# A convolution kernel with paired rows: the order of its two half sums, who normalises a few images, and where a denser pattern begins

## The chip, the cores and the metric

The kernel runs on one core of a Trainium2 chip. The metric is the device time of one execution in microseconds (us), median of several executions. All runs told here were in the fast state of the machine, and fast runs are compared with fast runs. A ratio is the mean time of one kernel's fast runs over the mean time of the other's fast runs of the same rounds, so it is not quite the ratio of the medians that are quoted. Where parts of the span are compared, the times are from one profiled execution of each kernel.

## The reference, cut to what matters

160 images of 128 channels and 32 x 32 pixels are normalised in groups of four channels, convolved 3 x 3 with weights of five sets (quantised on the fly), and added to the input.

```python
w = (v1 + v2).reshape(OUT_CH * N, IN_CH, K, K)          # two-step quantised U
...
act = jax.lax.conv_general_dilated(xb, w, window_strides=(1, 1),
          padding=[(1, 1), (1, 1)], feature_group_count=N, ...)
...
x = x + _L0_conv_ref(_gn(x), L0_conv_U)                 # _gn: 32 groups, eps 1e-5
```

## The kernel before

The precision of fp16 products is restored by two parts, a high and a low one, of each normalised image. Rows are taken in pairs, so that some products serve two rows: the sum half (`m[:, 0]`) and the difference half (`m[:, 1]`) of an image are multiplied first, into two banks of PSUM (the memory that TensorE writes its products to). A tile, below, is one buffer as the program allots it; here one tile, m, holds both banks. ScalarE copies the difference half out (`leave`), VectorE writes their sum and difference as the beginning of even and odd rows (`pairs`), and TensorE adds the remaining products on top (`rest_of_column`). "Combined" images form their row combinations in fp32 before they are split into parts; this saves TensorE products and costs VectorE work.

```python
def sums_of_pairs(self, i):
    m = self.m[i] = self.banks(self.ps_m, "m", i)      # ps_m has one buffer: two banks
    both = self.both(i)
    for a, kind in enumerate((self.SUM, self.DIFF)):
        for col in self.COLS:
            for j, (_, st) in enumerate(both):
                self.product(m[:, a], i, kind, st[:, a], col, ...)

def conv(self, i, on_the_way):
    if self.FIRST < i < self.imgs - 1:
        self.sums_of_pairs(i + 1)                      # the next image's halves
    ...                                                # then the rest of image i

def leave(self, i):
    m2 = self.evac.tile([self.P, self.H // 2, self.W], F32, tag="m2", name=f"m2_{i}")
    self.nc.scalar.copy(m2, self.m[i][:, 1])
    self.m[i] = self.m[i], m2

def pairs(self, i, between=lambda: None):
    m, m2 = self.m.pop(i)
    eo = self.eo[i] = self.banks(self.ps_eo, "eo", i)
    rows = eo.rearrange("p h (i a) w -> p (h i) a w", a=2)
    nc.vector.tensor_add(rows[:, :, 0], m[:, 0], m2)
    between()
    nc.vector.tensor_sub(rows[:, :, 1], m[:, 0], m2)

def combined(self, i):
    ...
    return (i - self.STEADY) % 7 % 2 == 0 if i < self.THIRDS else i % 3 != 1   # THIRDS = 126

def by_vector_too(self, i):                            # VectorE normalises in ScalarE's place
    if i < self.STEADY + 4 or i >= self.imgs or self.combined(i):
        return False
    return i >= self.THIRDS or (i - self.STEADY) % 7 == 3
```

Of the kernel before, what the change touches and what calls it, by code (L numbers as in the profile page):

```python
# [8 lines left out]
F32 = mybir.dt.float32  # L9
# [24 lines left out]
class Steps:  # L34


    def __init__(self, nc, pool):
        self.nc = nc
        self.pool = pool
        self.s1, self.s2, self.lift = (self.col(tag) for tag in ("s1", "s2", "lift"))  # L40
        self.parts1, self.parts2 = (
            tuple(self.col(tag + part) for part in ("r", "n", "nhi", "nlo"))
            for tag in ("s1", "s2")
        )
        self.far = self.col("fari", I32)
# [264 lines left out]
class Main:  # L310
# [25 lines left out]
    LOAD_LEAD = 18  # L336
    STEADY = 7
    BY_VECTOR = (8, 10, 11, 14, 19, 24, 29, 34)
    THIRDS = 126
    EARLY = 8  # L340
    FIRST = 3

# [4 lines left out]
    def __init__(self, tc, ctx, keep, x, u, out):  # L347
        nc = self.nc = tc.nc
        self.imgs, C, self.H, self.W = x.shape
        P = self.P = nc.NUM_PARTITIONS  # L350
        assert C == P and self.H * self.W == 1024
        self.per_set = self.imgs // N_SETS
        self.xv = x.rearrange("(b n) c h w -> n c b (h w)", n=N_SETS)
        self.ov = out.rearrange("(b n) c h w -> n c b (h w)", n=N_SETS)
        self.uv = u.rearrange("n (o i k) -> n o i k", o=C, k=TAPS)

        def pool(name, bufs, **kw):
            return ctx.enter_context(tc.tile_pool(name=name, bufs=bufs, **kw))

        self.const = pool("const", 1)  # L360
        self.qpool = pool("quant", 1)
        self.wpool = pool("weights", 2)
        self.upool = pool("u", 1)
        self.xpool = pool("x", 11)
        self.zpool = pool("z", 3)
        self.parts = pool("parts", 5)
        self.rows = pool("rows", 4)
        self.wide = pool("wide", 2)
        self.wide_parts = pool("wide_parts", 3)
        self.evac = pool("evac", 2)  # L370
        self.sums = pool("sums", 3)
        self.unread = pool("unread", 1)
        self.small = pool("small", 3)
        self.ps_eo = pool("ps_eo", 2, space=PSUM)
        self.ps_m = pool("ps_m", 1, space=PSUM)
        self.ps_stat = pool("ps_stat", 1, space=PSUM)
        self.ps_tr = pool("ps_tr", 1, space=PSUM)
        self.steps = Steps(nc, keep)
        self.chunks, self.z, self.hi, self.v, self.eo, self.m = {}, {}, {}, {}, {}, {}
        self.sum = {}  # L380
        self.wts = {}
        self.step = 0
        self.columns = []

        cuts = [0, 2, 4, 8, 12, 16, 20, *range(24, self.imgs + 1, 8)]
        self.groups = [range(a, b) for a, b in zip(cuts, cuts[1:])]
        self.group_of = {i: k for k, g in enumerate(self.groups) for i in g}
        self.stats = {}
# [135 lines left out]

    def by_vector_too(self, i):

        if i < self.STEADY + 4 or i >= self.imgs or self.combined(i):
            return False
        return i >= self.THIRDS or (i - self.STEADY) % 7 == 3

    def high_part(self, i):
        hi = self.parts.tile([self.P, self.H, self.W], MM, tag="hi", name=f"hi{i}")
# [3 lines left out]
    def combined(self, i):  # L536
# [3 lines left out]

        return (i - self.STEADY) % 7 % 2 == 0 if i < self.THIRDS else i % 3 != 1

# [94 lines left out]
                    skip_group_check=True,  # L637
                )

    def banks(self, pool, tag, i):  # L640
        return pool.tile([self.P, 2, self.H // 2, self.W], F32, tag=tag, name=f"{tag}{i}")

    def warm_up(self, count):


        zeros = self.los[3].rearrange("p h w -> p (h w)")
        if "warm" not in self.m:
            self.m["warm"] = self.banks(self.ps_m, "m", "warm")
        for _ in range(count):
            self.nc.tensor.matmul(  # L650
                self.m["warm"][:, 0].rearrange("p i w -> p (i w)"), zeros[:, :128],
                zeros[:, :512], start=True, stop=True,
            )

    def direct_hi(self, i, col):

        if i not in self.eo:
            self.eo[i] = self.banks(*((self.ps_eo, "eo") if i < 2 else (self.ps_m, "m")), i)
        self.taps(i, (self.hi[i], 0), col, self.eo[i], False)

    def direct_lo(self, i, col):
# [19 lines left out]

    def sums_of_pairs(self, i):

        m = self.m[i] = self.banks(self.ps_m, "m", i)
        both = self.both(i)
        for a, kind in enumerate((self.SUM, self.DIFF)):
            for col in self.COLS:
                for j, (_, st) in enumerate(both):
                    self.product(
                        m[:, a], i, kind, st[:, a], col,  # L690
                        col == self.COLS[0] and j == 0,
                        col == self.COLS[-1] and j == len(both) - 1,
                    )
# [30 lines left out]
    def leave(self, i):  # L724

        m2 = self.evac.tile([self.P, self.H // 2, self.W], F32, tag="m2", name=f"m2_{i}")
        self.nc.scalar.copy(m2, self.m[i][:, 1])  # L727
        self.m[i] = self.m[i], m2

    def pairs(self, i, between=lambda: None):  # L730


        nc = self.nc
        m, m2 = self.m.pop(i)
        eo = self.eo[i] = self.banks(self.ps_eo, "eo", i)
        rows = eo.rearrange("p h (i a) w -> p (h i) a w", a=2)
        nc.vector.tensor_add(rows[:, :, 0], m[:, 0], m2)  # L737
        between()
        nc.vector.tensor_sub(rows[:, :, 1], m[:, 0], m2)  # L739

    def by_hand(self, i):

# [336 lines left out]
```

## Time and profile before

| | before |
|---|---|
| median of 3 runs | 1057.07 us |
| span of the profiled run | 1053.8 us |
| TensorE / VectorE / ScalarE busy | 91 / 90 / 84% |
| images 17 to 24, profiled | 53.1 us |
| images 24 to 126 | 633.0 us, 6.21 an image |
| images 126 to 146 | 124.0 us |
| images 146 to 159 | 82.8 us |

Images are counted by ScalarE's copies of the difference half, one per image from image 3 on: "images 17 to 24" runs from the copy of image 17 to that of image 24. No engine is full, and the waits between them form a ring; the prediction shows the lines and reads them.

### The profile page before, as it was taken

How to read it: one execution, taken by the hardware profiler on the slowest of the kernel's cores; microseconds unless marked ns; L12 is line 12 of the kernel's file. 1: busy time of each engine (PE TensorE's matmuls, PEld its weight loads, DVE VectorE, ACT ScalarE, POOL GpSimd, SP SyncE). 2: the span in 40 equal slices, each digit the busy share in tenths (PEclk: the TensorE clock that was granted, in tenths of full speed). 3: DMA queues.
4: the chain of work that ended last, by engine and by line, in shares of the span. 5: the costliest groups of instructions: out<-in, count | busy, mean ns of one | idle time of the engine just before them, and what ended most of it. 6: DMA issues, size and time to landing. Idle time of an engine off the chain costs nothing.

```text
span 1053.8 us, 16029 instructions
## 1 busy us (share of the span) xinstructions
PE 955.8 (91%) x5935; PEld 574.3 (54%) x5935; DVE 943.6 (90%) x1264; ACT 883.2 (84%) x1202; POOL 439.8 (42%) x603
## 2 busy tenths in 40 slices
PE   1989998799999899999999999999999999898996
PEld 1445555455655556555555555555555555555554
DVE  7999997998899999889999998899999988889885
ACT  4879897789889998998998989988999888877451
POOL 3446653343515271635343544416162623243430
PEclk9999999899999999999999999999999999999999
DMA  9438899789999989999899999999999899997764
GB/s 361 172 101 240 239 241 264 205 230 239 280 257 244 258 242 264 258 278 268 257 241 261 251 258 256 278 255 242 264 264 254 238 262 260 252 242 200 178 160 143
DMA packets 67287, 254.42 MB, mean 241 GB/s; under 512 B 5248, under 2 KB 5248, under 8 KB 67200
## 3 DMA queue, kind: packets, MB, share of 16 engines
q1 hardware_dynamic: 45168, 173.09, 48.6%
q0 software_dynamic: 22032, 80.23, 39.4%
q8 instruction: 48, 0.79, 0.3%
q14 instruction: 39, 0.32, 0.1%
HBM read 89.19 MB, written 83.89 MB: 164 GB/s over the span
## 4 chain that ended last, share of the span: by engine, by line
PE 45%; DVE 33%; ACT 11%; issue 4%; POOL 4%; DMA 2%; SPq 0%; POOLq 0%; ACTq 0%; DVEq 0%
PE m L669 20%; PE eo L631 16%; PE eo L669 6%; DVE vl L584 6%; DVE eo L737 5%; DVE eo L739 5%; DVE v L567 4%; ACT vh L578 3%; ACT junk L199 3%; DVE v L570 3%; DVE v L573 2%; ACT m L727 2%; DVE lo L591 2%; DMA xt<-sum 1%; ACT sum L753 1%
## 5 line engine op out<-in xcount | busy, mean ns | idle before, releaser
L669 PEld LDWEIGHTS <-wt 128*128 128x128 f16 x4464 | 432.8, 98 | 311.8 <-DVE eo L739 74.9
L766 POOL DMA_DIRECT2D xt<-sum x153 | 138.3, 904 | 443.3 <-ACT sum L753 433.7
L631 PE MATMUL eo<-hi,wt 128*128 128x496 f16 (+3 forms) x1224 | 292.4, 376 | 1.1 <-ACT wt L477 0.6
L669 PE MATMUL m<-vh,wt 128*128 128x512 f16 x546 | 209.9, 384 | 60.3 <-DVE eo L739 60.2
L584 DVE SCALAR_TENSOR_TENSOR vl<-v,rstd,vh 128x2048 f16<-128x2048 f32 x91 | 213.6, 2347 | 0.4 <-ACT vh L578 0.3
L669 PE MATMUL eo<-vh,wt 128*128 128x256 f16 (+1 forms) x1092 | 209.3, 273 | 0.0
L669 PE MATMUL eo<-vl,wt 128*128 128x256 f16 (+1 forms) x1092 | 209.3, 273 | 0.0
L669 PE MATMUL m<-vl,wt 128*128 128x512 f16 x546 | 209.3, 383 | 0.0
L631 PEld LDWEIGHTS <-wt 128*128 128x128 f16 x1296 | 126.4, 99 | 124.2 <-ACT wt L477 1.8
L578 ACT ACTIVATE vh<-v,rstd 128x2048 f16<-128x2048 f32 x91 | 182.7, 2007 | 4.9 <-POOL v L557 4.0
L737 DVE TENSOR_TENSOR eo<-m,m 128x512 f32<-128x512 f32 x157 | 109.2, 696 | 82.3 <-ACT m L727 82.0
L753 ACT ACTIVATE sum<-eo 128x1024 f32<-128x1024 f32 x153 | 154.6, 1011 | 26.4 <-PE eo L669 25.6
L192 ACT ACTIVATE junk<-xt 128x1024 f16<-128x1024 f32 x152 | 160.7, 1057 | 17.3 <-DMA xt<-in_x_dram 14.3
L199 ACT ACTIVATE junk<-xt,mv 128x1024 f16<-128x1024 f32 x152 | 173.8, 1143 | 0.2
L727 ACT COPY m<-m 128x512 f32<-128x512 f32 x157 | 91.4, 582 | 96.0 <-PE m L669 95.2
L669 PE MATMUL eo<-rows,wt 128*128 128x248 f16 (+1 forms) x792 | 119.1, 273 | 0.0
L739 DVE TENSOR_TENSOR eo<-m,m 128x512 f32<-128x512 f32 x157 | 108.8, 693 | 1.2
L567 DVE TENSOR_TENSOR v<-xt 128x960 f32<-128x960 f32 x91 | 104.7, 1150 | 0.0
L669 PE MATMUL m<-rows,wt 128*128 128x496 f16 (+1 forms) x396 | 96.5, 380 | 0.8 <-DVE eo L739 0.8
L591 DVE TENSOR_TENSOR lo<-z,hi 128x1024 f16<-128x1024 f32 x69 | 84.5, 1224 | 0.7 <-POOL twice L244 0.7
L557 POOL TENSOR_SCALAR v<-xt,ngm 128x32 f32<-128x32 f32 x91 | 82.5, 907 | 0.0
L556 POOL TENSOR_SCALAR v<-xt,ngm 128x32 f32<-128x32 f32 x91 | 80.3, 883 | 0.0
(112 smaller groups left out, 895.4 us busy)
## 6 DMA issues: line engine op xcount, KB each, us to landing
xt<-in_x_dram SPq DMA_DIRECT2D x78, 1024.0 KB, 8.9
out_dram<-xt SPq DMA_DIRECT2D x78, 1024.0 KB, 5.1
xt<-sum POOLq DMA_DIRECT2D x153, 512.0 KB, 6.7
range<-in_L_conv_U_dram SPq DMA_DIRECT2D x4, 576.0 KB, 7.8
u<-in_L_conv_U_dram SPq DMA_DIRECT2D x4, 576.0 KB, 11.8
xt<-in_x_dram SPq DMA_DIRECT2D x4, 512.0 KB, 10.2
out_dram<-xt SPq DMA_DIRECT2D x3, 512.0 KB, 2.7
u<-in_L_conv_U_dram SPq DMA_DIRECT2D x2, 288.0 KB, 3.0
```

The source lines that it names most:

```text
L192: self.nc.scalar.activation(junk, image, ACTF.Copy, scale=-1.0 / image.shape[1], accum_out=self.mv[:, j, 0:1],)
L199: self.nc.scalar.activation(junk, image, ACTF.Square, bias=self.mv[:, j, 0:1], accum_out=self.mv[:, j, 1:2],)
L567: nc.vector.tensor_sub(v[:, W:last], x[:, : last - W], x[:, 2 * W :])
L578: self.nc.scalar.mul(vh, self.v[i], st.rstd[:, j])
L584: self.nc.vector.scalar_tensor_tensor(vl, self.v[i], st.rstd[:, j], self.hi[i], ALU.mult, ALU.subtract)
L631: nc.tensor.matmul(target[:, h, r0 - h0 : r1 - h0, c0:c1], self.wts[n, col][:, k, :], tile[:, s0 : s0 + r1 - r0, c0 + dw : c1 + dw], start ...
L669: self.nc.tensor.matmul(target[:, :, c0:c1], self.wts[n, col][:, kind, :], source[:, :, c0 + dw : c1 + dw], start=start, stop=stop, skip_g ...
L727: self.nc.scalar.copy(m2, self.m[i][:, 1])
L737: nc.vector.tensor_add(rows[:, :, 0], m[:, 0], m2)
L739: nc.vector.tensor_sub(rows[:, :, 1], m[:, 0], m2)
L753: nc.scalar.mul(self.sum[i], eo, 0.5)
L766: self.nc.gpsimd.dma_start(self.image(i), self.sum.pop(i), accum_op=ALU.add)
```

## The change

Its intent, as one reads it from the diff: the two banks of m become one lasting tile, so that no new buffer is allotted for each image, and the difference half is multiplied first. The copy can then run while the sum half is multiplied, and the next difference half can begin once the copy is through. Beside it, two parts of the schedule: images that begin a statistics group are normalised by ScalarE, and so are all the remaining ones from image 146; and the pattern of two combined images in three begins at image 146, not 126.

```diff
-    THIRDS = 126
+    THIRDS = 146
...
+        self.pair = self.ps_m.tile([P, 2, self.H // 2, self.W], F32, tag="m", name="m")
...
-        if i < self.STEADY + 4 or i >= self.imgs or self.combined(i):
+        if not self.STEADY + 4 <= i < self.THIRDS or (i - self.STEADY) % 7 != 3:
             return False
-        return i >= self.THIRDS or (i - self.STEADY) % 7 == 3
+        return i != self.groups[self.group_of[i]].start
...
-        m = self.m[i] = self.banks(self.ps_m, "m", i)
+        m = self.pair
         both = self.both(i)
-        for a, kind in enumerate((self.SUM, self.DIFF)):
+        for a, kind in ((1, self.DIFF), (0, self.SUM)):
...
-        self.nc.scalar.copy(m2, self.m[i][:, 1])
+        self.nc.scalar.copy(m2, self.pair[:, 1])
...
-        nc.vector.tensor_add(rows[:, :, 0], m[:, 0], m2)
+        nc.vector.tensor_add(rows[:, :, 0], m1, m2)          # m1 = self.pair[:, 0]
```

More of the change, by code (lines that the diff above doesn't have):

```diff
@@ L378, in __init__ @@
         self.steps = Steps(nc, keep)
-        self.chunks, self.z, self.hi, self.v, self.eo, self.m = {}, {}, {}, {}, {}, {}
+        self.pair = self.ps_m.tile([P, 2, self.H // 2, self.W], F32, tag="m", name="m")
+        self.chunks, self.z, self.hi, self.v, self.eo, self.m2 = {}, {}, {}, {}, {}, {}
         self.sum = {}
@@ L638, in taps, with bank_pair @@
                 )
-    def banks(self, pool, tag, i):
-        return pool.tile([self.P, 2, self.H // 2, self.W], F32, tag=tag, name=f"{tag}{i}")
+    def bank_pair(self, i):
+        return self.ps_eo.tile([self.P, 2, self.H // 2, self.W], F32, tag="eo", name=f"eo{i}")
     def warm_up(self, count):
         zeros = self.los[3].rearrange("p h w -> p (h w)")
-        if "warm" not in self.m:
-            self.m["warm"] = self.banks(self.ps_m, "m", "warm")
         for _ in range(count):
             self.nc.tensor.matmul(
-                self.m["warm"][:, 0].rearrange("p i w -> p (i w)"), zeros[:, :128],
+                self.pair[:, 0].rearrange("p i w -> p (i w)"), zeros[:, :128],
                 zeros[:, :512], start=True, stop=True,
@@ L657, in direct_hi @@
         if i not in self.eo:
-            self.eo[i] = self.banks(*((self.ps_eo, "eo") if i < 2 else (self.ps_m, "m")), i)
+            self.eo[i] = self.bank_pair(i) if i < 2 else self.pair
         self.taps(i, (self.hi[i], 0), col, self.eo[i], False)
@@ L726, in leave @@
         m2 = self.evac.tile([self.P, self.H // 2, self.W], F32, tag="m2", name=f"m2_{i}")
-        self.nc.scalar.copy(m2, self.m[i][:, 1])
-        self.m[i] = self.m[i], m2
+        self.nc.scalar.copy(m2, self.pair[:, 1])
+        self.m2[i] = m2
     def pairs(self, i, between=lambda: None):
         nc = self.nc
-        m, m2 = self.m.pop(i)
-        eo = self.eo[i] = self.banks(self.ps_eo, "eo", i)
+        m1, m2 = self.pair[:, 0], self.m2.pop(i)
+        eo = self.eo[i] = self.bank_pair(i)
         rows = eo.rearrange("p h (i a) w -> p (h i) a w", a=2)
-        nc.vector.tensor_add(rows[:, :, 0], m[:, 0], m2)
+        nc.vector.tensor_add(rows[:, :, 0], m1, m2)
         between()
-        nc.vector.tensor_sub(rows[:, :, 1], m[:, 0], m2)
+        nc.vector.tensor_sub(rows[:, :, 1], m1, m2)
     def by_hand(self, i):
```

## The prediction

> **What bounds the kernel now.** I read the busy shares first, then the waits of the steady stretch, then one turn of the loop in the timeline, then the three late stretches, and last the half-clock stretch near the start. In the fences the page comes first, then the waits of 201.8 to 834.8 us (images 24 to 126), then the timeline, then busy time by stretch.
>
> ```profile
> PE 955.8 (91%) x5935; PEld 574.3 (54%) x5935; DVE 943.6 (90%) x1264; ACT 883.2 (84%) x1202; POOL 439.8 (42%) x603
> L739 DVE TENSOR_TENSOR eo<-m,m 128x512 f32<-128x512 f32 x157 | 108.8, 693 | 1.2
> L521 DVE TENSOR_SCALAR z<-xt,rstd,shift 128x1024 f32<-128x1024 f32 x27 | 21.9, 812 | 3.9 <-POOL shift L242 3.9
> ```
>
> ```profile
> DVE eo L737 <- ACT m L727: 49.6, 56, 1.7
> ...
> ACT m L727 <- PE m L669: 37.3, 52, 1.6
> ...
> PE m L669 <- DVE eo L739: 32.4, 25, 1.7
> ```
>
> ```profile
> 407.45 0.57 ACT L727 COPY m<-m 128x512 f32<-128x512 f32 x1
> ...
> 408.06 0.70 DVE L737 TENSOR_TENSOR eo<-m,m 128x512 f32<-128x512 f32 x1 [0.34 <-ACT m L727]
> ...
> 409.00 0.69 DVE L739 TENSOR_TENSOR eo<-m,m 128x512 f32<-128x512 f32 x1
> ...
> 409.74 0.39 PE L669 MATMUL m<-vh,wt 128*128 128x512 f16 x1 [1.39 <-DVE eo L739]
> ```
>
> ```profile
> 150.00:200.00 50.00, 41.07 (x239) 23.47 (x237) 42.47 (x65) 37.85 (x52) 17.37 (x25) 0.90 0.94 262
> ...
> 201.80:834.80 633.00, 598.13 (x3762) 362.45 (x3761) 582.06 (x764) 579.26 (x789) 276.53 (x365) 1.00 0.95 253
> 834.80:958.80 124.00, 112.23 (x724) 69.93 (x723) 108.83 (x125) 107.07 (x144) 39.33 (x62) 1.00 0.94 249
> 958.80:1053.80 95.00, 81.50 (x526) 50.66 (x523) 72.72 (x84) 40.00 (x42) 28.85 (x36) 0.98 0.61 167
> ```
>
> No engine is full: TensorE, VectorE and ScalarE are at 94, 92 and 92% of the long stretch, and the DMA engines at 0.95. The waits close a ring. TensorE waits to write m until VectorE's second pair operation has read it; VectorE waits for ScalarE's copy of half of m; ScalarE waits for TensorE to finish that half. The timeline shows one turn: copy, add, subtract, and only then the first matmul of the next m, 1.39 us late. So a latency ring through one pair of PSUM banks binds, with all engines close behind it. In the steady stretch there are two such stops of 1.0 to 1.7 us in every seven images, which take 43.7 us (successive large pieces of the chain begin at 299.59, 343.34 and 387.10 us); in the later pattern of three images, 18.8 us, one of 1.6 to 1.8 us.
>
> **What the Trainium skill says.** "PSUM — Partial Sum Buffer", section "PSUM bank collisions raise a hardware error", asks that accesses be guarded by bank and quadrant. The two halves of m are 512 fp32 columns each, one bank each, so the sum half and the difference half may be released separately. The trace of before shows them released together: the first matmul of m waits for the last reader of either. "Perfetto Trace Analysis", section "Identifying the Most-Contended Engine", calls a repeating gap a sign of too little PSUM for the next tile; the repeating stop agrees. "DMA: Bandwidth & Descriptors", section "Issuing engines are not separate DMA queues": all transfers share 16 engines; the share of 0.95 is the warning here. "TensorE: Matmul & The Clock Gate", section "What's actually happening": an idle window of about 3.4 us halves the clock. In the 150 to 200 us window the granted clock is 0.90 and two runs of twelve product matmuls take 4.45 and 4.13 us in the chain instead of 2.61 or 2.77; the gaps near them are 2.8 and 6.0 us, so the trace agrees roughly.
>
> **The change part by part.** *Order and buffer.* Durations are start to start in the timeline and the chain. TensorE: m takes 2.6 us for a combined image (12 matmuls), 1.3 for another (6); the rest takes 2.6 (24 half matmuls) or 5.15 (three times 1.27 + 0.44). Per seven images (4 combined, 3 not): 4 x 5.2 + 3 x 6.45 = 40.15 us, and 40.8 busy with the statistics' and weights' matmuls. VectorE: low part of a combined image 2.26, its combining 1.06 + 0.66 + 0.60 = 2.3; low part and row combinations of another 1.13 + 0.60 + 0.33 + 0.33 = 2.4; pairs 1.25; a normalising 0.8; quantising about 0.8 per image. Per seven: 4 x 5.8 + 3 x 3.65 + 0.8 + 5.6 = 40.5.
>
> Let L be the time from the end of an image's m to the end of its pairs. Before, L is at least the copy (0.65) plus pairs (1.4), 2.05, and TensorE stops when L exceeds the rest of the image before: 2.6 or 5.15. Carrying L through the seven images (VectorE's work minus TensorE's is +1.2, +1.55, -2.15, +1.55, +0.15, -0.9, -1.0) gives two stops, 0.65 and 1.15. Two are seen, larger (2.9 together), since waits and handovers are not in these sums. After, difference first: the copy runs under the sum half, so L starts at 1.4; and the next difference half needs only the copy, so L may reach the rest plus half an m: 3.25 to 6.45. The same walk gives L of 2.6, 4.15, 2.0, 3.55, 3.7, 2.8, 1.8 against limits 3.9, 5.8, 3.9, 5.8, 3.9, 6.45, 3.25. No stop remains, by 0.2 us in the tightest place. The floor is then TensorE's 598 us over 102 images, 5.86 an image, for 6.21 now. VectorE during quantising (40.8 of each 43.7) is just as full[...]; I take 5.97. Saved: 102 x 0.24 = 24 us.
>
> *Thirds from image 146.* Images 126 to 145 become 11 combined and 9 not, for 13 and 7: TensorE gains 2 x 1.2 = 2.4 us of work, VectorE loses some. They now take 124.0 us / 20 = 6.20; the ring's loss there (11.8 us of TensorE waits) disappears. At 5.95 each: 5 us saved. From 146 the ring was 7.75 (TensorE) + 4.7 (m, copy, pairs) + 6.0 (combining, low part, pairs) = 18.45, seen as 18.8 per three images. After: 7.75 + 2.65 + 6.0 = 16.4, under TensorE's 16.9 to 17.1. Some 1.6 us per three images over 13 images: 6 us after the unhelped last image.
>
> *First of a group.* Images 24, 80 and 136 move from VectorE (0.8 us) to ScalarE (1.24 us). Vector normalisings go from 27 to 16, scalar ones from 42 to 55; from 146 on ScalarE has no measuring, so it is free. Image 24's vector normalising waits 3.9 us for its shift, and behind it stands TensorE's gap of 6.0 us and a half-clock run (4.13 for 2.6). That stop goes; with less ring before it, 7 us for images 3 to 24, which otherwise are bound by VectorE's quantising.
>
> Sum: 24 + 5 + 6 + 7 = 42 us; 1057 - 42 = 1015, which I round to 1016.
>
> **The rivals.** *DMA becomes the bound.* For: share 0.95; each load lands late, by my subtraction of landing from first use a median of some 3.5 us ahead, several with 0.1; a chunk's buffer comes back six images after its last residual, so 0.24 us an image takes 1.4 us off that margin. Transfers alone are, an estimate from q1's 48.6% and q0's 39.4% of 1053.8 us over 160 images, 5.8 us an image, part of it two packets overlapping on one engine. Against: ScalarE waits for loads only a few times so far. It would hold 6.05 to 6.1 an image: 1030. *The order of release does not split by bank* and the difference still waits for the subtraction: only the copy is hidden, a third to half of the gain, 1036 to 1040. Against: the diff replaces a buffer allotted anew per image by one lasting tile, which only makes sense if halves are tracked apart. *ScalarE becomes the bound*: 579 us busy of 633, plus 13 more normalisings, but 11 of these lie where it has slack or no measuring; a further 1 to 3 us. *Everything overlaps to the floor*: 5.86 an image, 1003.
>
> **Range and chances.** Mostly the ring goes and something at 96 to 98% takes its place. I predict 1016 us, with 1003 to 1036 for 8 times in 10. Faster by over 2% means under 1035.9; chance 0.87. Within 2%: 0.12. Slower: 0.01, as no part adds work to a full engine beyond 2.4 us.
>
> **What would show it.** Right: TensorE's wait on the pairs' second operation falls from 61 us to under 15; the wait of the pairs' first on ScalarE's copy from 82 to under 30, its place partly taken by a wait on TensorE's sum half; seven images take 41.3 to 42.2 us; three in the tail about 17.2; the half-clock stretch near 190 us is gone. Wrong: first uses of loads that wait for DMA by tens of microseconds (first rival); difference matmuls that still begin right after the subtraction (second rival); long gaps at images 24 and 80 that remain.

## The result, and the profile after

The changed kernel takes 1042.09 us (median of 4) against 1056.12 for the kernel before; ratio 0.987, 95% interval 0.9843 to 0.9896. It is 1.3% faster where I had 3.9%, and outside my range of 1003 to 1036 us.

The waits of images 24 to 126 in the changed kernel (columns: total us, times, longest us), to be held against those of the same images before:

```profile
DVE eo L738 <- ACT m L728: 49.5, 57, 1.7
...
ACT m L728 <- PE m L670: 38.8, 51, 1.6
...
PE m L670 <- DVE eo L740: 32.6, 26, 1.7
```

Before they were 49.6, 37.3 and 32.4 us. Nothing has moved. The same turn of the loop, in the changed kernel's timeline (start, duration, engine, line; in brackets the idle time before and what ended it):

```profile
398.76 0.57 ACT L728 COPY m<-m 128x512 f32<-128x512 f32 x1
...
399.37 0.70 DVE L738 TENSOR_TENSOR eo<-m,m 128x512 f32<-128x512 f32 x1 [0.34 <-ACT m L728]
...
400.32 0.69 DVE L740 TENSOR_TENSOR eo<-m,m 128x512 f32<-128x512 f32 x1
...
401.06 0.39 PE L670 MATMUL m<-vh,wt 128*128 128x512 f16 x1 [1.39 <-DVE eo L740]
```

The product at 401.06 us is now the first of the *difference* half, which nobody reads but the copy at 398.76. Still it starts after the subtraction, 1.39 us late, as before. Busy time by stretch shows where the 14 us came from; first the kernel before, then the changed one (columns: stretch, length, busy time of TensorE, weight loads, VectorE, ScalarE and GpSimd with their instructions, granted clock, share of the DMA engines, GB/s). The four stretches are images 17 to 24, 24 to 126, 126 to 146, and the rest.

```profile
148.78:201.84 53.06, 44.13 (x261) 25.64 (x259) 44.34 (x66) 40.31 (x56) 18.59 (x27) 0.90 0.94 264
201.84:834.81 632.97, 598.10 (x3762) 362.42 (x3761) 582.06 (x764) 579.26 (x789) 276.54 (x365) 1.00 0.95 253
834.81:958.84 124.03, 112.26 (x724) 69.92 (x723) 108.83 (x125) 107.11 (x144) 39.32 (x62) 1.00 0.94 249
958.84:1053.80 94.96, 81.46 (x526) 50.66 (x523) 72.72 (x84) 39.96 (x42) 28.85 (x36) 0.98 0.61 168
```

```profile
146.76:192.90 46.14, 41.10 (x261) 24.88 (x260) 43.24 (x65) 41.26 (x56) 20.15 (x27) 1.00 0.94 254
192.90:826.09 633.19, 598.15 (x3763) 362.53 (x3761) 580.76 (x763) 581.65 (x792) 272.62 (x365) 1.00 0.95 257
826.09:943.98 117.89, 114.33 (x725) 70.15 (x723) 101.36 (x120) 112.56 (x150) 37.19 (x58) 1.00 0.99 262
943.98:1038.90 94.92, 81.42 (x525) 50.78 (x523) 70.30 (x81) 45.03 (x46) 25.60 (x36) 0.99 0.61 168
```

Images 17 to 24 gain 6.9 us, images 126 to 146 gain 6.1, and the long stretch, where I had expected most, gains nothing: 632.97 against 633.19. The remaining 2 us of the spans lie before image 3, where the profiled runs of one and the same start differ by that much (the copy of image 3 comes at 56.9 to 58.9 us in the runs below, whatever was changed). VectorE's vector normalisings are 16 for 27, ScalarE's 55 for 42, as counted in advance.

So the theory to test (A): the two halves are parts of one tile, and the built program releases this tile as a whole, so the order of the products cannot matter. A list of the waits in the built program of the changed kernel says the same:

```
first weights of the difference half, image 81  wait for  the subtraction of the pairs of image 80
first product of the difference half, image 81  waits for  the copy of image 80
copy of the difference half, image 80           waits for  the last product of the SUM half, image 80
```

The rival (B): the reversal works, and transfers or VectorE take the gain away.

### The profile page after: what moved, and what is told of

Same layout as the page of the kernel before. It is cut to its first block, busy times and chain, and to the rows that moved or that the text cites. A ratio compares the mean times of both kernels' runs of the same rounds, so it can differ in the third digit from the quotient of the medians.

```text
span 1038.9 us, 16017 instructions
## 1 busy us (share of the span) xinstructions
PE 953.6 (92%) x5935; PEld 573.6 (55%) x5935; DVE 931.0 (90%) x1253; ACT 897.1 (86%) x1215; POOL 433.7 (42%) x599
## 3 DMA queue, kind: packets, MB, share of 16 engines
q1 hardware_dynamic: 45168, 173.09, 49.1%
q0 software_dynamic: 22032, 80.23, 39.9%
## 4 chain that ended last, share of the span: by engine, by line
PE 42%; DVE 29%; ACT 12%; issue 7%; POOL 5%; DMA 5%; SPq 0%; POOLq 0%; ACTq 0%; DVEq 0%
PE m L670 18%; PE eo L634 15%; PE eo L670 7%; DVE eo L738 4%; DVE vl L587 4%; DVE eo L740 4%; ACT vh L581 4%; DVE v L570 3%; ACT junk L199 3%; DMA xt<-in_x_dram 3%; DVE v L573 2%; DVE v L576 2%; DMA xt<-sum 2%; ACT m L728 2%; DVE lo L594 2%
## 5 line engine op out<-in xcount | busy, mean ns | idle before, releaser
L634 PE MATMUL eo<-hi,wt 128*128 128x496 f16 (+3 forms) x1260 | 300.9, 375 | 1.1 <-ACT wt L479 0.6
L670 PE MATMUL m<-vh,wt 128*128 128x512 f16 x534 | 203.4, 381 | 48.2 <-DVE eo L740 48.0
L587 DVE SCALAR_TENSOR_TENSOR vl<-v,rstd,vh 128x2048 f16<-128x2048 f32 x89 | 208.7, 2345 | 1.2 <-ACT vh L581 1.1
L670 PE MATMUL eo<-vl,wt 128*128 128x248 f16 (+1 forms) x1068 | 204.7, 273 | 0.0
L670 PE MATMUL eo<-vh,wt 128*128 128x248 f16 (+1 forms) x1068 | 204.6, 273 | 0.0
L670 PE MATMUL m<-vl,wt 128*128 128x512 f16 x534 | 202.9, 380 | 0.0
L581 ACT ACTIVATE vh<-v,rstd 128x2048 f16<-128x2048 f32 x89 | 178.6, 2007 | 4.6 <-POOL v L560 3.7
L670 PE MATMUL eo<-rows,wt 128*128 128x248 f16 (+1 forms) x816 | 122.7, 273 | 0.0
L670 PE MATMUL m<-rows,wt 128*128 128x496 f16 (+1 forms) x408 | 99.4, 380 | 0.8 <-DVE eo L740 0.8
L560 POOL TENSOR_SCALAR v<-xt,ngm 128x32 f32<-128x32 f32 x89 | 81.5, 916 | 0.0
L559 POOL TENSOR_SCALAR v<-xt,ngm 128x32 f32<-128x32 f32 x89 | 76.4, 858 | 0.0
```

The lines of the kernel that those rows point to most:

```text
L581: self.nc.scalar.mul(vh, self.v[i], st.rstd[:, j])
L587: self.nc.vector.scalar_tensor_tensor(vl, self.v[i], st.rstd[:, j], self.hi[i], ALU.mult, ALU.subtract)
L634: nc.tensor.matmul(target[:, h, r0 - h0 : r1 - h0, c0:c1], self.wts[n, col][:, k, :], tile[:, s0 : s0 + r1 - r0, c0 + dw : c1 + dw], start ...
L670: self.nc.tensor.matmul(target[:, :, c0:c1], self.wts[n, col][:, kind, :], source[:, :, c0 + dw : c1 + dw], start=start, stop=stop, skip_g ...
```

## The experiments

**E1, the reversal alone.** The changed kernel with the schedule of before.

```diff
-    THIRDS = 146
+    THIRDS = 126
...                       # and by_vector_too as it was before
```

> The kernel before with the difference half multiplied first into one lasting tile, and nothing else of the change. Theory A (the two halves are one tile and are released together, whatever the order of the products): nothing moves, ratio to before 0.998 to 1.002, about 1056 us, and TensorE's wait on the pairs' second operation stays near 61 us, the wait of the pairs' first operation on the copy near 82 us. Theory B (the reversal works as predicted but something else, transfers or VectorE, takes up the gain): these two waits fall by half or more and a new wait of the same size stands in their place, at an unchanged time. Theory C (the reversal gives part of the gain by itself): ratio 0.97 to 0.99.

Measured: 1056.65 us, ratio 1.0008 (0.9993 to 1.0024). Images 24 to 126 take 633.2 us. The waits of its whole span are those of before (61.0 and 82.0 us there):

```profile
DVE eo L737 <- ACT m L727: 82.5, 81, 2.1
...
PE m L669 <- DVE eo L739: 61.1, 41, 6.0
```

The reversal by itself gives nothing that the runs can tell from zero, and no new wait stands in place of an old one. This is A, not B.

**E2, group starts to ScalarE alone**, in the kernel before.

```diff
+        if i == self.groups[self.group_of[i]].start:
+            return False
         return i >= self.THIRDS or (i - self.STEADY) % 7 == 3
```

> The kernel before with images that begin a group (24, 80, 136) normalised by ScalarE, and nothing else. By the trace of the changed kernel images 17 to 24 take 6.9 us less; if this part alone makes that, the ratio is 0.992 to 0.995 (about 1049 us) and images 17 to 24 take 46 us for 53. If the reversal were behind it, the ratio is 0.999 to 1.001.

Measured: 1049.62 us, ratio 0.995 (0.993 to 0.9969). Images 17 to 24 take 46.2 us for 53.1, everything else is unchanged to 1 us:

```profile
148.20:194.50 46.30, 41.25 (x262) 25.02 (x261) 43.40 (x65) 41.42 (x57) 20.16 (x27) 1.00 0.94 253
```

The granted clock is 1.00 here where it was 0.90: the gap of 6.0 us behind image 24's wait is gone, and no half-clock run follows.

**E3, the later pattern alone**, in the kernel before: `THIRDS = 146`, with VectorE still normalising from there on.

> The kernel before with two of three combined from image 146 in place of 126, and nothing else (from 146 on VectorE still normalises). If the pattern alone shortens images 126 to 146, these 20 take 118 us for 124 and the ratio is 0.993 to 0.996 (about 1050 us). If my predicted cause was right (the ring of waits removed there by the reversal), they stay at 123 to 124 us and the ratio is 0.998 to 1.002.

Measured: 1049.02 us, ratio 0.9943 (0.9927 to 0.996). Images 126 to 146 take 117.7 us for 124.0:

```profile
832.90:950.60 117.70, 114.27 (x725) 70.08 (x723) 102.51 (x122) 111.75 (x150) 37.08 (x58) 1.00 0.98 262
```

So the pattern alone makes that gain. E1 to E3 multiply to 0.990 (1.0008 x 0.995 x 0.9943), just above the interval of the whole change (0.9843 to 0.9896), by less than what each of the three is uncertain by (up to 0.002); in the profiled runs the sum 6.9 + 6.3 stands against 6.9 + 6.1.

**E4, the two halves in two tiles.** The changed kernel, each half a tile of one bank. (Image 2, which borrows the pair for its direct convolution, adds its residual in two halves.)

```diff
-        self.pair = self.ps_m.tile([P, 2, self.H // 2, self.W], F32, tag="m", name="m")
+        self.pair = [
+            self.ps_m.tile([P, self.H // 2, self.W], F32, tag=f"m{a}", name=f"half{a}_")
+            for a in range(2)
+        ]
...
-                        m[:, a], i, kind, st[:, a], col,
+                        m[a], i, kind, st[:, a], col,
```

> The changed kernel with the two halves in two tiles of one bank each, in place of the two halves of one tile. Theory A: now the difference half waits only for the copy and the copy only for the difference half; the ring goes, seven images take 41.3 to 42.2 us for 43.4 and the whole 1010 to 1025 us, ratio to before 0.955 to 0.972. Theory B: seven images stay above 43 us and the time at 1036 to 1043 us, since the ring was not what the time hung on.

Measured: 1012.82 us (six runs, 1008.02 to 1017.48), correct, ratio 0.9588 (0.9554 to 0.9621). The timeline of a turn (half__127 is the difference half, half__126 the sum half):

```profile
413.37 0.58 ACT L733 COPY m<-half__127 128x512 f32<-128x512 f32 x1
...
415.80 0.38 PE L675 MATMUL half__127<-vh,wt 128*128 128x512 f16 x1
...
416.71 0.70 DVE L745 TENSOR_TENSOR eo<-half__126,m 128x512 f32<-128x512 f32 x1
...
417.46 0.38 PE L675 MATMUL half__126<-vh,wt 128*128 128x512 f16 x1
```

The difference half of the next image begins 0.9 us before the subtraction does, and only the sum half comes after it. By stretch (24 to 126, 126 to 146, the rest):

```profile
192.16:812.27 620.11, 598.28 (x3733) 362.69 (x3732) 580.13 (x762) 575.21 (x793) 295.61 (x364) 0.99 0.97 262
812.27:928.28 116.01, 116.01 (x738) 71.92 (x737) 101.44 (x121) 111.98 (x151) 39.08 (x59) 1.00 0.99 265
928.28:1014.60 86.32, 79.30 (x518) 50.34 (x516) 70.03 (x81) 44.49 (x46) 25.32 (x36) 0.99 0.67 184
```

From image 126 to 146 TensorE is busy 116.01 of 116.01 us. In the long stretch it is busy 96%, and a wait that was small before (2.7 us, for loads) has grown:

```profile
DVE eo L743 <- ACT m L733: 29.2, 21, 4.6
...
ACT junk L192 <- DMA xt<-in_x_dram: 25.6, 15, 5.9
```

ScalarE now waits for loads 25.6 us where TensorE has 21.8 us of idle time. A is confirmed by the time and the ratio: the ring was what the time hung on. Seven images take 42.6 us, which misses A's 41.3 to 42.2 by a little, and my floor of 5.86 us an image was not reached in the long stretch: 620.1 / 102 = 6.08. This is where something of B shows, once the ring is gone. One caution: E4's six runs fall into two groups, 1008.0 to 1009.3 and 1016.3 to 1017.5 us, and the profiled one is of the upper group; what parts the groups is not known, so the 6.08 may be high by some of these 8 us.

**E5, two tiles, but the sum half first.**

```diff
-        for a, kind in ((1, self.DIFF), (0, self.SUM)):
+        for a, kind in ((0, self.SUM), (1, self.DIFF)):
```

> Two tiles as in the split kernel, but the sum half multiplied first again. If it takes both (separate release and the difference first), the sum half still waits for the subtraction and the copy still comes after both halves: the ring stays, seven images take 43 to 43.8 us and the ratio to before is 0.98 to 0.99 (about 1042 us). If separate release alone breaks the ring, the ratio is 0.955 to 0.97.

Measured: 1044.6 us, ratio 0.9896 (0.9877 to 0.9915). The ring is back whole (images 24 to 126: 633.3 us):

```profile
DVE eo L743 <- ACT m L733: 49.5, 54, 2.0
...
ACT m L733 <- PE half__127 L675: 38.4, 51, 1.6
...
PE half__126 L675 <- DVE eo L745: 32.7, 26, 1.7
```

So it takes both: the order without separate tiles gives nothing (E1), separate tiles without the order give nothing beyond the schedule parts (E5), and together they take off 32 us more (1044.6 to 1012.8, E4).

**E6, the split with the schedule of before**: E4 with `THIRDS = 126` and `by_vector_too` as it was.

> The split with the difference first, and without the other two parts of the change: two of three combined from 126, all group starts that fell to VectorE left there. If the gain of the two scheduling parts (7 and 6 us beside the ring) stays whole once the ring is gone, this is 13 us slower than the split kernel, about 1026 us. If the pattern from 126 was slow only because of the ring, it loses only the 4 to 7 us of image 24, about 1018 us, ratio 0.962 to 0.967.

Measured: 1009.21 us (four runs, 1004.11 to 1017.45), ratio 0.9543 (0.9518 to 0.9569). It is not slower than E4, and neither of the two expected times, 1026 and 1018, is met. Images 126 to 146 take 117.8 us for 116.0:

```profile
811.60:929.40 117.80, 115.12 (x741) 72.19 (x740) 108.65 (x126) 106.85 (x145) 40.78 (x63) 1.00 0.98 262
```

Images 17 to 24 take 49.6 for 48.0 (where I had expected a loss of 4 to 7), and the rest agrees to 1.5 us. The profiled run is the longest of the four. The later start of the denser pattern, worth 6.3 us with the ring, is worth 1.8 without it: a repair of the ring in one stretch, which the repair of its cause makes nearly needless. E4 and E6 are both about 4% faster than the kernel before and about 3% faster than the changed kernel; their intervals overlap by a little and I don't rank them.

**E7, loads ahead of stores in the queue**, in the kernel of E4.

```diff
-            self.store(i - 2)
             while loaded * NB < min(self.imgs, i + self.LOAD_LEAD):
                 self.load(loaded)
                 loaded += 1
+            self.store(i - 2)
```

> The split kernel with each chunk's load issued ahead of the store of the same turn, not behind it (that store waits for an accumulation). Loads should land some 5 to 7 us earlier against their first use. If late loads are what keeps images 24 to 126 of the split kernel at 6.08 us, where TensorE's own work is 5.86, ScalarE's wait on loads falls from 37 us to under 15 and the time to 995 to 1006 us, ratio 0.943 to 0.953. If the transfers' bandwidth or another engine holds it, the wait moves elsewhere and the time stays at 1009 to 1016 us.

Measured: 1014.08 us, ratio 0.9608 (0.9581 to 0.9634). The time fits the second branch: no gain. ScalarE's wait on loads falls only from 37.2 to 32.2 us; in images 24 to 126 it falls from 25.6 to 14.7, yet these still take 617.7 us for 620.1. The miss was in my step that loads would go out earlier: between a load's issue and its first use lie 9.4 us in the median for 10.9 in E4 (first uses from 250 to 800 us in the two traces). The queue's own waits of 250 to 800 us, first E4, then E7:

```profile
SPq L786 <- DMA xt<-sum: 486.0, 56, 13.6
```

```profile
SPq L413 <- DMA out_dram<-xt: 448.4, 43, 13.3
SPq L786 <- DMA xt<-sum: 31.0, 9, 9.3
```

In E4 the queue waits at a store for its accumulation. In E7 it waits at a load for the store that frees its buffer, and the store after it goes out later in turn. The chain accumulate, store, load of one buffer is the same, only the place of waiting moved; a load cannot go out before its buffer is free. (A chunk is the buffer of two images that one load fills. A twelfth did not fit the memory, so more buffers could not be tried.)

**E8, half the store** (a wrong result on purpose: the second half of each image is not written; all waits stay), in the kernel of E4.

```diff
-                self.ov[n, :, b - NB + 1 : b + 1, :], self.chunks[i // NB]
+                self.ov[n, :, b - NB + 1 : b + 1, :512], self.chunks[i // NB][:, :, :512]
```

> The split kernel storing only the first half of each image (wrong result on purpose; all waits as they were). By the mean packet time of the load and store queue a store costs about 1.4 us of all 16 engines per image, so this takes away some 0.7 us an image of 5.8. If the transfers hold the split kernel back, by bandwidth or by landing late, the time falls to 990 to 1004 us; if an engine does, it stays at 1009 to 1016 us.

Measured: 1002.43 us, ratio 0.95 (0.9476 to 0.9524), and images 24 to 126 take 607.0 us for 620.1:

```profile
192.20:799.20 607.00, 595.06 (x3734) 362.66 (x3733) 580.04 (x762) 576.01 (x793) 289.60 (x364) 1.00 0.90 224
```

With less to move (224 GB/s for 262) TensorE reaches 98% of this stretch. ScalarE's wait on loads there falls from 25.6 to 8.8 us. So in E4 the transfers are most of what keeps the long stretch from TensorE's floor. (The 13 us between the two profiled runs overstate it: the medians differ by 10.4 us, and E4's faster group lies 6 us above E8's median.) Whether by their rate or by the length of one buffer's chain, E7 and E8 do not tell apart: E8 shortens both.

## Why the prediction was wrong

- **What bounds the kernel: right.** The ring that I read from the waits binds. Removing it takes 43 us off with the schedule parts (E4) and 46 us without them (E6), and E4's 1012.8 us is near the 1016 that I had predicted for the change. That nearness is partly luck: in the profiled run the long stretch gives 12.9 us of my 24, images 126 to 146 give 8.0 for 5, the later ones 10 for 6, and those before 24 give 9.5 for 7.
- **The step that failed** is in "Order and buffer": "the copy runs under the sum half, so L starts at 1.4; and the next difference half needs only the copy". It took for granted that the built program releases the two banks apart. The second rival doubted it for the next difference half alone, still had the copy hidden, and expected 1036 to 1040. In fact neither is released apart (E1: 61.1 and 82.5 us of waits, ratio 1.0008). What "PSUM — Partial Sum Buffer" in the Trainium skill asks for in its section "PSUM bank collisions raise a hardware error", a guard by bank and quadrant, says what is safe; I read it as what the program does. The argument "which only makes sense if halves are tracked apart" was an argument from intent, not from a trace. The 24 us for the long stretch measured 0.
- **Two readings beside it were wrong.** I wrote that the trace of before shows the two halves released together. It cannot: the first product of that kernel writes the sum half, whose own last reader is the subtraction, so it waits for it either way, as E5 does with two tiles (32.7 us). And my walk with L stopped after seven images. It ends at 1.8, above its start of 1.4; carried into the next seven, L reaches 4.1 where 3.9 is the limit, and later rounds keep a stop of 0.4 us by the same sums, so "no stop remains" did not follow.
- **Thirds from 146: the size right (5 predicted, 6.1 and 6.3 measured), the reason wrong.** I had credited the reversal; E3 has the gain without it. The walk with L explains it without any change of order, though this is argued, not shown: VectorE has no weights to quantise in these images, so its 0.8 us an image fall away, L of the seven-image pattern peaks at 3.2 against 5.15, and stays under 2.6 where 2.6 is the limit, while the three-image pattern keeps its ring of 18.45. The shift takes images 126 to 146 out of the ring (TensorE's wait there falls from 11.8 to 3.4 us) although TensorE has 2.1 us more work there (114.33 for 112.26). I didn't redo the walk without quantising; it would have given this.
- **From 146 on: 6 us predicted, 0.3 measured** by images 146 to 159. The same failed step: the 18.45 us ring of that pattern is untouched. E4 takes 10 us off these images (72.8 for 82.8), so there the estimate for a broken ring was low.
- **First of a group: right in kind, the size partly chance.** 7 us predicted, 6.9 measured in the profiled runs, and E2 shows that this part alone does it. But before, twelve products after the gaps of 2.75 and 6.02 us took 4.3 and 4.0 us; in E2 and the changed kernel gaps of 2.75 and 2.1 us remain and the products behind them take 2.6. The same 2.75 us gap is followed by slow products in one run and not in another. E3, which runs the code of before in these images, settles what that is worth: its products after the 2.75 us take 2.6, those after 6.03 us take 4.0, and images 17 to 24 take 51.5 us for 53.1:

```profile
148.23:199.71 51.48, 42.54 (x261) 25.24 (x260) 44.38 (x66) 40.34 (x55) 18.60 (x27) 0.93 0.96 269
```

  So 1.6 of the 6.9 us are chance of one run, and over all its runs E2 gains about 5 us (ratio 0.995). "TensorE: Matmul & The Clock Gate" in the Trainium skill, section "What's actually happening", has the clock judged in free-running windows of about 3.4 us. That one and the same gap has two outcomes agrees with windows that run freely; that a gap of 2.75 us, shorter than a window, is followed by slow products at all does not agree with a whole idle window being needed, and stays open.
- **DMA as a rival: not what stopped the change, but what comes next.** It holds E4's profiled run at 6.08 us an image, within the 6.05 to 6.1 that I gave this rival, and I had given it too little weight inside my sum of 5.97. Loads that landed 3.6 us ahead of their first use in the median (first uses from 250 to 800 us) land 0.9 us ahead in E4.

## What to carry to other kernels

A gain from releasing a buffer earlier needs two things that are easy to take for one: an order of work in which the early release helps, and a buffer that the built program does release on its own. Look up in the list of waits what the first writer waits for, and give parts that are to be released apart their own tiles. And when a schedule parameter gains in one stretch, ask which wait it avoids there: with the ring gone, the shifted pattern here lost most of its worth.

## What the Trainium skill lacked or had wrong

- "PSUM — Partial Sum Buffer", section "PSUM bank collisions raise a hardware error", gives the unit in which accesses must be guarded, the bank and quadrant. It does not warn that a program may guard more coarsely: with both banks in one tile TensorE's wait stays at 61.1 us (E1), with a tile for each bank and the reversed order the time falls by 4.6% on the schedule of before (E6).
- "Perfetto Trace Analysis", section "Identifying the Most-Contended Engine", says to optimise the engine of highest occupancy first, with its own caveat for TensorE. Here three engines stood at 92 to 94% of the long stretch, and the gain lay in the ring of waits between them, not in any of their work: TensorE's work from image 24 to 126 is 598.1 us before and 598.3 in E4. What fits is the page's next section, "Optimization Strategy", with its remark on consistent bubbles, though more buffers were not what was needed.
- "DMA: Bandwidth & Descriptors", section "SDMA does more than copy", names the accumulating copy without a rate. In the changed kernel the accumulating queue's 22032 packets take 39.9% of 16 engines' 1038.9 us, 301 ns each on average, and the other's 45168 packets 49.1%, 181 ns each; the accumulation moves a third of the bytes (80 of 254 MB) in 45% of the packets' time.
